# A softmax factor moved: from the product's columns into the exponentials, in a two-layer cross-attention kernel

## The chip, the cores and the metric

The kernel runs on one core of a Trainium2 chip. A core has five engines that work side by side, each through its own list of instructions in order: TensorE (PE in the profile, with its weight loads as PEld), VectorE (DVE), ScalarE (ACT), GpSimd (POOL) and SyncE (SP, which here only issues DMAs). The metric is the device time of one execution in microseconds (us).

## The reference, cut to what matters

Two cross-attention layers, over 4 batches of 1024 rows of 512 features, with a context of 1024 rows of 384 features. All in fp32. Layer 0, which the change touches, has 16 heads of 64:

```python
h = layernorm(x) * gamma + beta
Q, K, V = h @ Wq, context @ Wk, context @ Wv        # 16 heads of 64
attn = softmax(Q @ K^T, axis=-1) * 64 ** -0.5       # the scale stands after the softmax
x = x + (attn @ V) @ Wo + bo
```

Layer 1 has 16 heads of 32, an RMS norm, rotary embeddings and normed queries and keys, `softmax(q @ k^T * sqrt(32)) @ v`, and adds its projection to x in the same way. The change doesn't touch it.

## The kernel before, in words

The outer loop runs over the batches. Within a batch, layer 0 goes through 8 pairs of heads (p), and for each pair through 8 tiles of 128 query rows (i): 64 steps a batch, 256 in all. `Attention0.step` (L381) is one step. Two steps, an even and an odd one, make a block (BQ = 2): 32 blocks a batch, 128 in all.

A step works for the two heads of the pair (j = 0, 1), with 1024 context rows each:

1. `scores` (L372): four matmuls of 64x512 into two PSUM tiles "s" of 128 queries x 1024 context rows. There are two such tiles in all, so the next step's scores need this step's exponentials to have read them.
2. Maxima (L395, VectorE) and exponentials (L396, ScalarE) into e, with the row sums l gathered on the way.
3. A first filling (L398): up to 1.8 us of other work from a list of units (below).
4. Transposes of e in place on VectorE (L401), which turn 32x32 squares; then, in an odd step, 16 DMAs (L407, SP's queue) that carry the squares of the block to their places in eT, so that context rows lie on the partitions. e and eT have two buffers each, and each buffer holds a block.
5. The reciprocals of the row sums (L408), 128x2.
6. In an even step, if two blocks are waiting: `product` (L443) of the older one, 32 matmuls of the values with eT into a PSUM bank av, and then one VectorE multiplication (L456) of av by the factors.
7. A second filling with the rest of the step's share (L416).

The product has heads' features on its partitions and queries along its columns, while the reciprocals have the queries on the partitions. So the factors are turned: `factors` (L418) spreads the reciprocals, times 64 ** -0.5, over 64 columns each on GpSimd (rb), and `factors_turned` (L431) transposes rb on TensorE into a bank rT and copies that to the place of the result (vals) on ScalarE (L441).

The order of work is written out by hand. `Units` holds a list of small pieces of other work, each with a cost in microseconds: projections of the next pairs (k, q, v; matmuls on L158, evacuated by ScalarE copies on L130), output projections that VectorE adds to x (L301), norms, layer 1's first keys with their rotation (L499 to L504) in pairs 6 and 7. `fill` issues pieces until their costs reach what the step is given; the loop (L798 to L809) spreads what is left evenly over the remaining steps, and takes 3.9 (AV) off a step that issues a product. While the first filling runs, rotations are held back (`holds["posts"]`) and issued after the transposes (`flush`). The PSUM banks for fillings, rT and av are four, taken in turn (`bank`).

After a batch's last step two blocks are still without their product. Their products stand in the list of work between layer 0 and layer 1 (L827 to L835), with output projections, the norm of layer 1 and the first queries and keys.

## Time and profile before

| what | value |
|---|---|
| time, median of 3 runs | 2983.13 us (2977.34 to 2984.37) |
| the profiled execution | 2979.04 us, span 2976.8 us |
| TensorE clock granted | 0.997 |
| layer 0 of batch 0, pairs 1 to 5 (96.2 to 364.7 us) | 268.5 us, 40 steps |
| L396 exponential, 128x1024, ACT, x512 | 1109 ns each |
| L395 maximum, 128x1024, DVE, x512 | 1218 ns each |
| L401 transpose, 128x1024, DVE, x512 | 1223 ns each |
| L441 copy of the factors, 128x256, ACT, x128 | 372 ns each |
| L456 product with the factors, 128x256, DVE, x128 | 408 ns each |
| eT DMAs, 128 KB, SP's queue, x2048 | 2.4 us to landing |

A line of the timeline gives the start in us from the span's beginning, the duration, engine, source line, operation, what is written and read, and how many instructions were merged; in square brackets stands the idle time of the engine ahead of it, and what ended it. Instructions that follow one another without a wait overlap by about 0.1 us in the records, so two maxima of 1.22 us take 2.36. A line of the windows gives the stretch, its length, the busy time of each engine with its count of instructions, the clock, the DMA engines' share and GB/s.

### The profile page before, as it was taken

To read this page: it belongs to the slowest core of one execution; us is meant where nothing else is said; L and a number is where in the kernel's file an instruction comes from. 1 tells how busy PE (TensorE), PEld (TensorE's weight loads), DVE (VectorE), ACT (ScalarE), POOL (GpSimd) and SP (SyncE) were. 2 spreads that over 40 slices of the span, in tenths; PEclk is the share of its full clock that TensorE was granted. 3 is DMA by queue.
4 is the path that set the end of the run, shared out by engine and by line. 5 is a ranking of instruction groups with operands and counts; after the bars stand their busy time and mean duration, and the time that the engine had idled before them with its cause. 6 is when DMAs were issued, how large, how long until landed. Compare 5 with 4: busy or idle time off the path is not lost.

```text
span 2976.8 us, 60525 instructions
## 1 busy us (share of the span) xinstructions
PE 2914.2 (98%) x24748; PEld 1541.9 (52%) x24748; DVE 2228.5 (75%) x2824; ACT 1429.5 (48%) x2265; POOL 416.5 (14%) x392
## 2 busy tenths in 40 slices
PE   8999999999999999999999999999999999999998
PEld 5544546555544555655554454555455455555544
DVE  4777795877777779587777777958767777795777
ACT  3444443656534444465644444446664444444664
POOL 0010012420000002232000000223100000023310
PEclk9999999999999999999999999999999999999999
DMA  5787674010388777301048887730104878772000
GB/s 146 169 197 180 158 178 114 21 35 25 74 200 196 183 161 178 95 21 35 25 95 213 183 177 169 166 84 21 35 25 117 209 176 182 167 171 66 2 2 30
DMA packets 177525, 348.49 MB, mean 117 GB/s; under 512 B 37600, under 2 KB 93152, under 8 KB 177248
## 3 DMA queue, kind: packets, MB, share of 16 engines
q1 hardware_dynamic: 175056, 343.43, 48.8%
q8 instruction: 196, 3.21, 0.5%
q10 hardware_dynamic: 2192, 1.19, 0.1%
q14 instruction: 81, 0.66, 0.1%
HBM read 67.64 MB, written 8.39 MB: 26 GB/s over the span
## 4 chain that ended last, share of the span: by engine, by line
PE 82%; DVE 8%; DMA 3%; SPq 3%; ACT 2%; issue 1%; POOL 1%; ACTq 0%; DVEq 0%
PE s L372 15%; PE av L449 13%; PE po L158 10%; PE s L597 7%; PE pv L158 7%; PE av L636 6%; PE pqT L158 6%; PE pkT L158 5%; PE q_p L158 3%; PE av L647 2%; SPq L407 2%; PE k_p L158 2%; DVE both L613 2%; DMA eT<-e 1%; PE rT L440 1%
## 5 line engine op out<-in xcount | busy, mean ns | idle before, releaser
L396 ACT ACTIVATE e<-s,m 128x1024 f32<-128x1024 f32 x512 | 565.6, 1109 | 666.7 <-DVE m L395 623.1
L395 DVE TENSOR_REDUCE m<-s 128x1 f32<-128x1024 f32 x512 | 602.6, 1218 | 321.4 <-PE s L372 321.4
L607 ACT ACTIVATE e<-s 128x1024 f32<-128x1024 f32 x512 | 496.5, 1022 | 315.3 <-PE s L597 300.2
L401 DVE STREAM_TRANSPOSE e<-e 128x1024 f32<-128x1024 f32 x512 | 606.6, 1223 | 46.9 <-ACT e L396 41.1
L372 PE MATMUL s<-qk 64*128 64x512 f32 x2048 | 520.5, 615 | 6.0 <-ACT e L396 5.3
L449 PE MATMUL av<-eT,v 128*64 128x256 f32 x4096 | 470.3, 382 | 7.8 <-DMA eT<-e 6.2
L613 DVE TENSOR_TENSOR both<-e 128x512 f32<-128x512 f32 x512 | 342.1, 699 | 128.9 <-ACT e L607 93.7
L449 PEld LDWEIGHTS av<-eT,v 128*64 128x64 f32 x4096 | 285.5, 137 | 205.3 <-issue 50.2
L372 PEld LDWEIGHTS s<-qk 64*128 64x128 f32 x2048 | 181.8, 186 | 262.6 <-issue 188.5
L597 PE MATMUL s<-q,k 32*128 32x256 f32 x4096 | 304.7, 401 | 5.8 <-ACT q L524 2.7
L597 PEld LDWEIGHTS s<-q,k 32*128 32x128 f32 x4096 | 190.8, 184 | 149.6 <-ACT e L607 71.4
L158 PE MATMUL po<-wo,vals 128*128 128x512 f32 x512 | 239.6, 601 | 2.5 <-ACT v L130 2.5
L158 PE MATMUL pqT<-hT,w 128*128 128x512 f32 (+1 forms) x800 | 241.3, 597 | 0.7 <-ACT hT L255 0.7
L441 ACT COPY vals<-rT 128x256 f32<-128x256 f32 x128 | 47.7, 372 | 327.4 <-PE rT L440 327.4
L301 DVE TENSOR_TENSOR x<-x,po 128x512 f32<-128x512 f32 x200 | 133.6, 678 | 82.6 <-PE po L158 82.6
L158 PEld LDWEIGHTS pv<-w,cT 128*128 128x128 f32 (+1 forms) x2400 | 176.7, 152 | 30.3 <-issue 27.2
L158 PE MATMUL pv<-w,cT 128*128 128x128 f32 (+1 forms) x2400 | 186.5, 275 | 0.0
L158 PE MATMUL pkT<-cT,w 128*128 128x512 f32 (+1 forms) x600 | 182.7, 601 | 1.0 <-ACT cT L130 1.0
L617 DVE TENSOR_TENSOR both<-both 128x1024 f32<-128x1024 f32 x128 | 159.7, 1248 | 4.4
L158 PEld LDWEIGHTS po<-wo,vals 128*128 128x128 f32 x512 | 90.9, 190 | 106.5 <-issue 102.3
L158 PEld LDWEIGHTS pqT<-hT,w 128*128 128x128 f32 (+1 forms) x800 | 85.9, 151 | 112.2 <-issue 105.9
L636 PE MATMUL av<-e,v 128*32 128x256 f32 x2048 | 137.0, 385 | 0.0
(461 smaller groups left out, 2669.9 us busy)
## 6 DMA issues: line engine op xcount, KB each, us to landing
eT<-e SPq DMA_DIRECT2D x2048, 128.0 KB, 2.4
xr<-in_x_dram SPq DMA_DIRECT2D x32, 256.0 KB, 4.0
x<-in_x_dram SPq DMA_DIRECT2D x32, 256.0 KB, 4.0
wo<-in_Wo_dram SPq DMA_DIRECT2D x16, 512.0 KB, 4.0
out_dram<-x SPq DMA_DIRECT2D x32, 256.0 KB, 2.7
w<-in_Wq_dram SPq DMA_DIRECT2D x31, 256.0 KB, 3.9
c<-in_ctx_dram SPq DMA_DIRECT2D x32, 192.0 KB, 3.8
wkv<-in_wkv_dram SPq DMA_DIRECT2D x16, 384.0 KB, 3.3
```

The source lines that it names most:

```text
L158: nc.tensor.matmul(o[rr], lhsT[:, rr], rhs, start=start, stop=stop)
L301: nc.vector.tensor_add(xt[t], xt[t], pp[0])
L372: nc.tensor.matmul(sc[j][:, kb * 512 : (kb + 1) * 512], pr["qT"][r[j], i * P : (i + 1) * P], pr["kT"][r[j], kb * 512 : (kb + 1) * 512], st ...
L395: nc.vector.tensor_reduce(m[:, j : j + 1], sc[j], AX.X, ALU.max, negate=True)
L396: nc.scalar.activation(e[j], sc[j].rearrange("p (g s) -> p g s", g=4), AF.Exp, bias=m[:, j : j + 1], accum_out=l[:, j : j + 1])
L401: nc.vector.transpose(e[j], e[j])
L449: nc.tensor.matmul(av[r[j], :W].rearrange("p (t a i) -> p t a i", t=BQ, a=4), pr["v"][:, k, r[j]], eT[:, j, :, :, k * 32 : (k + 1) * 32], ...
L597: nc.tensor.matmul(sc[j // 2][:, j % 2, c, :], kT[rr, g, k * P : (k + 1) * P], qT[rr, g, qb * WQ : (qb + 1) * WQ], start=True, stop=True,)
L607: nc.scalar.activation(e, sc[u], AF.Exp, scale=float(np.sqrt(np.float32(HD1))))
L613: nc.vector.tensor_add(self.both[:, kk, 2 * u : 2 * u + 2, :], es[u][:, :, 0, :], es[u][:, :, 1, :])
L617: nc.vector.tensor_add(self.both[:, 0], self.both[:, 0], self.both[:, kk])
L636: nc.tensor.matmul(self.av[rr, 0, :], v[g][:, 2 * kk + c, rr], es[j // 2][:, j % 2, c, :], start=first and c == 0, stop=end and c == 1,)
```

## The change

The factors are no longer turned. In each step the reciprocals are taken for each head apart (128x1), ScalarE multiplies each head's exponentials in place by them, and only then do the transposes come. `factors` and `factors_turned` go, with the tiles rb and rT; the bank av is scaled by the constant 64 ** -0.5 by VectorE, in the new `results`, after the transposes. The product of a block stands in the odd step instead of the even one, right behind its scores and ahead of the first filling; the plan of the fillings follows it (AV is taken off odd steps), and other work joins the list at i == 4 instead of 3. After a batch's last step, the two last products come later in the list: the first behind the first half of the output projection and the norm's statistics, the second behind the norm's turning, the first queries and two pieces of keys.

```diff
         def step(self, p, i, pr, us):
...
-            if i % BQ == 0 and len(self.blocks) == 2:
-                self.factors_turned()
+            if i % BQ == BQ - 1 and len(self.blocks) == 2:
+                self.product()
...
+            li = sb.tile([P, 2], F32, tag="li", bufs=3, name=f"li_{n}")
...
             for j in range(2):
+                nc.vector.reciprocal(li[:, j : j + 1], l[:, j : j + 1])
+                nc.scalar.mul(e[j], e[j], li[:, j : j + 1])
+            for j in range(2):
                 nc.vector.transpose(e[j], e[j])
+            self.results()
             flush()
...
-            nc.vector.reciprocal(self.li[:, i % BQ, :], l)
             if i % BQ == BQ - 1:
-                eT = eT.rearrange("p a (t h) s -> p h t a s", h=2)
-                self.blocks.append((p, i // BQ, pr, eT, self.li))
-            elif self.blocks:
-                if len(self.blocks) == 2:
-                    self.product()
-                self.factors()
+                self.blocks.append((p, i // BQ, pr, eT.rearrange("p a (t h) s -> p h t a s", h=2)))
...
         def product(self):
...
-            nc.vector.tensor_mul(o, av[:, :W], o)
+            self.av = av[:, :W], pr["vals"][:, q * W : (q + 1) * W]
+
+        def results(self):
+            if self.av is not None:
+                av, o = self.av
+                nc.vector.tensor_scalar_mul(o, av, HD0**-0.5)
+                self.av = None
...
-                if i == 3:
+                if i == 4:
                     work.add(other)
...
-                now = 0.0 if i % 2 or len(att.blocks) < 2 else AV
+                now = AV if i % 2 and len(att.blocks) == 2 else 0.0
...
-                todo = work.total() + left + later + AV * (n // 2)
+                todo = work.total() + left + later + AV * ((n + 1) // 2)
...
-        att.factors_turned()
-        work.add([(AV, second)] + flat(outs[:4]) + norms[0]["stats"])
-        work.add(k1[0][0] + [(0.2, att.factors_turned)] + norms[0]["apply"] + [(AV, att.product)])
-        work.add(norms[0]["turn"] + q[0][0] + k1[1][0] + k1[0][2] + flat(outs[4:]) + q[0][2])
+        work.add(flat(outs[:4]) + norms[0]["stats"] + [(AV, product)] + k1[0][0] + norms[0]["apply"])
+        work.add(norms[0]["turn"] + q[0][0] + k1[1][0] + [(AV, product)] + k1[0][2] + flat(outs[4:]) + q[0][2])
         work.drain()
```

More of the change, by code (lines that the diff above doesn't have):

```diff
@@ L383, in step @@
             sc = self.scores(p, i, pr)
-            if i % BQ == 0 and len(self.blocks) == 2:
-                self.factors_turned()
+            if i % BQ == BQ - 1 and len(self.blocks) == 2:
+                self.product()
             m = sb.tile([P, 2], F32, tag="m", bufs=3, name=f"m_{n}")
             l = sb.tile([P, 2], F32, tag="l", bufs=3, name=f"l_{n}")
+            li = sb.tile([P, 2], F32, tag="li", bufs=3, name=f"li_{n}")
             if i % BQ == 0:
                 self.e = sb.tile([P, 4, BQ * 2, S // 4], F32, tag="e", bufs=2, name=f"e0_{n}")
-                self.li = sb.tile([P, BQ, 2], F32, tag="li", bufs=4, name=f"li_{n}")
             e = [self.e[:, :, i % BQ * 2 + j, :] for j in range(2)]
@@ L407, in step, with product @@
                         nc.sync.dma_start(eT[32 * g : 32 * (g + 1), q], self.e[32 * q : 32 * (q + 1), g])
-            nc.vector.reciprocal(self.li[:, i % BQ, :], l)
             if i % BQ == BQ - 1:
-                eT = eT.rearrange("p a (t h) s -> p h t a s", h=2)
-                self.blocks.append((p, i // BQ, pr, eT, self.li))
-            elif self.blocks:
-                if len(self.blocks) == 2:
-                    self.product()
-                self.factors()
-            self.u.fill(us - min(us, 1.8))
-        def factors(self):
-            li = self.blocks[0][4]
-            self.rb = sb.tile([P, BQ, P], F32, tag="rb", bufs=2, name=f"rb_{self.blocks[0][:2]}")
-            nc.gpsimd.tensor_scalar(
-                self.rb.rearrange("p t (j d) -> p (t j) d", j=2),
-                li.rearrange("p t j -> p (t j)").unsqueeze(2).to_broadcast([P, 2 * BQ, HD0]),
-                HD0**-0.5,
-                0.0,
-                ALU.mult,
-                ALU.add,
-            )
-        def factors_turned(self):
-            p, q, pr = self.blocks[0][:3]
+                self.blocks.append((p, i // BQ, pr, eT.rearrange("p a (t h) s -> p h t a s", h=2)))
+            self.u.fill(us - min(us, 1.8))
+        def product(self):
+            p, q, pr, eT = self.blocks.popleft()
             W = BQ * P
@@ L436, in factors_turned @@
                 pr["vals"] = sb.tile([P, S], F32, tag="vals", bufs=4, name=f"vals0_{self.b}_{p}")
-            self.o = pr["vals"][:, q * W : (q + 1) * W]
-            rT = bank(f"rT_{self.b}_{p}_{q}")
-            for k in range(BQ):
-                nc.tensor.transpose(rT[:, k * P : (k + 1) * P], self.rb[:, k, :], ident)
-            nc.scalar.copy(self.o, rT[:, :W])
-        def product(self):
-            p, q, pr, eT, _ = self.blocks.popleft()
-            o, W = self.o, BQ * P
             av = bank(f"av_{self.b}_{p}_{q}")
@@ L455, in product @@
                     )
-            nc.vector.tensor_mul(o, av[:, :W], o)
+            self.av = av[:, :W], pr["vals"][:, q * W : (q + 1) * W]
[3 more added lines that the diff above has]
+                nc.vector.tensor_scalar_mul(o, av, HD0**-0.5)
+                self.av = None
     TH = 2
@@ L825, in xattn_kernel, with product @@
         q1 = rotated_chains(qT1, xnT, NQ, lambda k: wq1[:, k, :], f"q1_{b}_1", tmp)
-        def second():
+        def product():
             att.product()
-            att.factors()
-        att.factors_turned()
-        work.add([(AV, second)] + flat(outs[:4]) + norms[0]["stats"])
-        work.add(k1[0][0] + [(0.2, att.factors_turned)] + norms[0]["apply"] + [(AV, att.product)])
-        work.add(norms[0]["turn"] + q[0][0] + k1[1][0] + k1[0][2] + flat(outs[4:]) + q[0][2])
+            att.results()
+        work.add(flat(outs[:4]) + norms[0]["stats"] + [(AV, product)] + k1[0][0] + norms[0]["apply"])
+        work.add(norms[0]["turn"] + q[0][0] + k1[1][0] + [(AV, product)] + k1[0][2] + flat(outs[4:]) + q[0][2])
         work.drain()
```

## The prediction

> **What bounds the kernel now.** First the page's busy times and its chain of work that ended last, then busy times by stage, then one step in order of time, because the change acts inside a step.

> Busy time, and the two lines of the chain:

> ```profile
> PE 2914.2 (98%) x24748; PEld 1541.9 (52%) x24748; DVE 2228.5 (75%) x2824; ACT 1429.5 (48%) x2265; POOL 416.5 (14%) x392
> ...
> PE 82%; DVE 8%; DMA 3%; SPq 3%; ACT 2%; issue 1%; POOL 1%; ACTq 0%; DVEq 0%
> PE s L372 15%; PE av L449 13%; PE po L158 10%; PE s L597 7%; PE pv L158 7%; PE av L636 6%; PE pqT L158 6%; PE pkT L158 5%; PE q_p L158 3%; PE av L647 2%; SPq L407 2%; PE k_p L158 2%; DVE both L613 2%; DMA eT<-e 1%; PE rT L440 1%
> ```

> TensorE sets the time; the factors' transposes (rT) are 1% of it. By stage, with batch 0's layer 0 cut into pairs 1 to 5 (40 steps), pair 6 and pair 7 (8 steps each); the columns are length, then the busy time of PE, PEld, DVE, ACT and POOL:

> ```profile
> 96.20:364.70 268.50, 267.87 (x1425) 136.59 (x1424) 204.48 (x231) 114.82 (x210) 17.53 (x27) 1.00 0.78 181
> 364.70:417.50 52.80, 52.80 (x271) 27.23 (x270) 46.64 (x61) 21.78 (x40) 10.06 (x10) 1.00 0.76 179
> 417.50:475.00 57.50, 56.18 (x295) 31.64 (x295) 48.72 (x62) 24.05 (x48) 10.06 (x10) 1.00 0.70 163
> ```

> A step takes 268.5/40 = 6.71 us with PE full and VectorE 76% busy: it has some 1.6 us of idle time in a step, in pair 6 only 0.8. One step of pair 4 in the timeline:

> ```profile
> 304.73 2.36 DVE L395 TENSOR_REDUCE m<-s 128x1 f32<-128x1024 f32 x2 [1.48 <-PE s L372]
> 306.05 1.11 ACT L396 ACTIVATE e<-s,m 128x1024 f32<-128x1024 f32 x1 [4.94 <-DVE m L395]
> 307.16 1.11 ACT L396 ACTIVATE e<-s,m 128x1024 f32<-128x1024 f32 x1
> 307.29 2.37 DVE L401 STREAM_TRANSPOSE e<-e 128x1024 f32<-128x1024 f32 x2 [0.20 <-ACT e L396]
> 308.25 1.07 ACT L130 COPY v<-pv 128x512 f32<-128x512 f32 x2
> 309.58 0.12 DVE L408 RECIPROCAL li<-l 128x2 f32<-128x2 f32 x1
> ...
> 312.81 2.35 DVE L395 TENSOR_REDUCE m<-s 128x1 f32<-128x1024 f32 x2 [1.22 <-PE s L372]
> ```

> The first transpose starts 2.56 us after the first maximum (R = 304.73), as the first exponential is done by the time the second maximum is. VectorE has finished the step's work at R+4.85 and then waits for the next scores. That wait is the cover which the change spends.

> [...] the trace has one table load, at the start, so the multiply brings none. [...] a square of 512 elements is 633 ns from SBUF (L229), 601 from PSUM (L497).

> **The change, part by part.**

> Multiply. 512 ACTIVATEs of 128x1024 with one pointer[...]. Bounds: 1.02 (L607, no pointer)[...]. That is 2.1 us more a step on ScalarE, which is busy 115 of 268 us in pairs 1 to 5: no throughput limit. But the multiply stands in ScalarE's order after both exponentials and after the evacuations of the step's first filling, and behind it, in VectorE's order, stand both transposes, the results, and the next step's maxima. The new period of VectorE, from R:
> - second exponential over and the next ACT instruction started: 308.25-304.73 = 3.52;
> - first multiply 1.13, then 0.04 to the waiting engine (the transpose at 307.29 began that long after the accumulator was read, 307.25): R+4.69;
> - both transposes until the next instruction, 309.58-307.29 = 2.29; the second multiply starts at R+4.56 and is over by R+5.69, when the first transpose still runs: R+6.98.

> So a step can't be shorter than 6.98 us, 2.13 later than before. The two 128x1 reciprocals lie in the gap, where they cost nothing; without it 0.1 us.

> On top of 6.98 comes what stands in that ring in the instruction order of the changed kernel. Evacuations ahead of the multiplies: 2 to 3 in a pair, 0.54 each (L130, two in 1.07), 1.3 a pair. Scaled results: 4 a pair at 0.33 (L456 now takes 0.41; 0.08 overlaps), 1.3. In pairs 0 to 5, about one addition of po after the transposes, 0.6 (L301 0.68, less overlap). Sum 55.8+3.2 = 59.0 a pair, 7.38 a step.
> Pair 6: 55.8, evacuations 0.5, results 1.3, six additions 3.5, two rotations of keys (five VectorE instructions after the transposes, 2.5 each) 5.1: 66.2. Pair 7: 55.8, 1.5, 1.3, 0.8 and 5.1: 64.5.

> PE does not stop this: its scores for the next step start once the exponentials have released PSUM, about R+3.6, and are ready at about R+5.4, 1.6 us before VectorE comes. PE has work of some 6.5 us a step (the 6.71 less half of a block's 0.37), so it idles.

> Against before. Batch 0: pair 0 is PE-bound at 69.9 us for 8 steps, stays so and gains 1 us. Pairs 1 to 5: 40 x (7.38-6.71) = 27. A later batch (pairs 0 and 1: 106.9 us, 2 to 5: 220.3): 48 steps in 327.2 = 6.82, 48 x 0.56 = 27. Pair 6: 66.2-52.8 = 13.4. Pair 7: 64.5-57.5 = 7. Four batches: 4 x (27+13.4+7) - 1 = 189.

> Removed: 256 transposes on PE, 0.37 us a block on the chain, 128 x 0.37 = 47 us; 128 ACT copies of 0.37, 128 POOL operations of 0.40, a VectorE product that becomes a scaling. PE's 47 us would come off the time if PE still set it; under the ring above they only lengthen PE's idle time, so I count nothing but the 1 us in pair 0.

> Product a step later. It now follows the scores of an odd step. Exponentials reach eT 2.1 us later, the product waits a step (7 us) longer: nothing. A block's 16 DMAs are issued in some 10 to 11 us (one block's in 11.38) and land 2.4 us after the last; then its e buffer may be written again, by the first exponential three steps on. From the end of the transposes that is 3 x 6.71 + 1.32 - 4.85 = 16.6 us before and 3 x 7.38 + 1.32 - 6.98 = 16.5 after: the late start and the longer steps cancel, and there are 3 to 4 us to spare as before. But 46 of the 512 exponentials waited for this in the trace of before, 31.3 us in all, and where PE set the pace that was partly hidden; in the ring it isn't. Between 0 and 31 us; taken 8. SP's queue holds the same issues in the same order, POOL loses the broadcast alone.

> Last products of a batch. The same PE work between layer 0 and 1, in another order: the first additions (6.9 us) and first keys come ahead of products that used to open the stage. The last transposes come 2.1 us later, but the last product has 21 us of PE work ahead of it, where it had 13. Squares and norm keep their cover (3.7+2.6 us). Between -2 and +2 a batch, taken 0. Layer 1 is untouched.

> The profiled execution took 2979.0 us (span 2976.8), 4 below the median: 2983+189+8 = 3180.

> **Rivals.**
> - A, shorter ring: multiply at L607's 1.02, half of the evacuations hidden because PSUM was ready earlier: 0.2 us x 248 steps = 50 less, 3130. For: the bounds. Against: the evacuation is in order ahead of the multiply whenever its data came.
> - B, longer ring: waits between engines add a quarter of a us, or PE's 1.6 us of lead is lost in steps with much filling: 0.25 x 248 = 60 more, 3240. For: PE's odd steps now hold scores and a product of 3.67 us ahead of any filling.
> - C, e buffer: the DMA engines are 78% busy in this stage, and blocks land too late in most cases, 1.5 us in two thirds of 120 blocks: +120, 3300. For: 46 waits already. Against: the spare time above.
> - D, the other side: VectorE's waits are covered and PE stays the bound: 2983-47 = 2936. It decides where the ring is under PE's 6.5 us, that is, if the multiply with its extras took below 0.4 us. Against: 1024 elements in that time would be twice the rate of any ACT row.
> - E, the scores' lead hides nearly all and both effects cancel: 2980.

> **How the numbers follow.** Forecast 0.60, A 0.17, B 0.12, C 0.06, D 0.03, E 0.02. The range takes in the forecast with its bounds, most of A and B: 3100 to 3245. Some 0.3% is what can be told from no change. Faster D, 0.03; same E, 0.02; slower the rest, 0.95.

> **What would show it.** Right: VectorE waits about 2 us before each first transpose, released by ACT's multiply; maxima no longer wait for scores; PE waits for exponentials at its scores in layer 0; steps of 7.4 us; pair 6 above 65; layer 1 unchanged. Wrong: transposes that start at R+2.6; a multiply well under 1 us; exponentials waiting on DMA in most blocks.

## The result, and the profile after

The changed kernel takes 3209.53 us (median; 3203.41 to 3212.41), the kernel before, beside it, 2983.75. The ratio is 1.0763, 95% interval 1.0745 to 1.0781: 226 us slower, where 197 were forecast. Its profiled execution has a span of 3208.5 us. One execution of the run e9_deferred_product_even below took 11913.12 us, some four times the others, and is left out of that run's median.

Busy times and the chain of work that ended last, of the changed kernel's page (its lines: maxima L397, exponentials L398, reciprocals L403, multiply L404, transposes L406, scaled results L438, scores L374):

```profile
PE 3063.8 (95%) x24492; PEld 1594.9 (50%) x24492; DVE 2277.3 (71%) x3080; ACT 1922.3 (60%) x2649; POOL 366.2 (11%) x264
...
PE 53%; DVE 21%; ACT 11%; SPq 6%; DMA 6%; issue 2%; POOL 1%; ACTq 0%; DVEq 0%
DVE e L406 10%; PE s L374 8%; PE s L580 7%; ACT e L398 7%; PE po L159 6%; PE av L426 6%; PE av L619 6%; SPq L413 6%; PE pv L159 5%; DMA eT<-e 4%; PE pqT L159 4%; DVE m L397 3%; ACT e L404 3%; PE q_p L159 3%; PE pkT L159 3%
```

TensorE's share of the chain fell from 82% to 53%; transposes, exponentials and multiplies took most of it, and the DMAs with their issue went from 6% to 12%. PE still reads 95% busy, though it has fewer instructions than before. The same 2048 score matmuls read 673.9 us busy in place of 520.5, and their weight loads wait 252.5 us for exponentials, where they waited 37.3. In pairs 1 to 5 of batch 0 the granted clock is 1.00 in both kernels, and these matmuls read 107.3 us busy in place of 80.1: some of PE's waiting stands inside what is called busy. A busy share alone would have shown little.

One step of pair 4 in the timeline of the changed kernel:

```profile
283.58 2.34 DVE L397 TENSOR_REDUCE m<-s 128x1 f32<-128x1024 f32 x2
284.82 1.11 ACT L398 ACTIVATE e<-s,m 128x1024 f32<-128x1024 f32 x1 [3.11 <-DVE m L397]
285.95 1.11 ACT L398 ACTIVATE e<-s,m 128x1024 f32<-128x1024 f32 x1
286.06 0.16 DVE L403 RECIPROCAL li<-l 128x1 f32<-128x1 f32 x1
...
287.06 2.17 ACT L404 ACTIVATE e<-e,li 128x1024 f32<-128x1024 f32 x2
287.19 0.16 DVE L403 RECIPROCAL li<-l 128x1 f32<-128x1 f32 x1 [0.97 <-ACT e L398]
...
288.23 2.37 DVE L406 STREAM_TRANSPOSE e<-e 128x1024 f32<-128x1024 f32 x2 [0.87 <-ACT e L404]
290.52 0.39 DVE L438 TENSOR_SCALAR vals<-av 128x256 f32<-128x256 f32 x1
290.83 1.21 DVE L397 TENSOR_REDUCE m<-s 128x1 f32<-128x1024 f32 x1
```

From the first maximum (283.58) the first multiply starts at +3.48, the first transpose at +4.65, and VectorE has done both at +6.94; then the results, and the next maxima at +7.25 with no wait in front. The forecast had +3.52, +4.69 and +6.98. The brackets are the change's price: VectorE waits 0.97 for the second exponential and 0.87 for the multiply. Over the whole run, from VectorE's waits:

```profile
DVE li L403 <- ACT e L398: 217.7, 243, 1.5
DVE e L406 <- ACT e L404: 173.9, 165, 3.3
...
DVE e L406 <- DMA eT<-e: 97.1, 91, 1.4
...
DVE m L397 <- PE s L374: 24.4, 13, 3.4
```

A line of the waits gives the total in us, how often, and the longest. The line that names a DMA is the multiply as well: in all 256 steps the first transpose starts 31 to 34 ns after the end of the first multiply, whichever of the two is named. Maxima wait 24.4 us for scores now; in the kernel before it was

```profile
DVE m L395 <- PE s L372: 321.4, 219, 5.2
```

The stages of batch 0, as the windows of the changed kernel (length, then busy PE, PEld, DVE, ACT, POOL, the granted clock, the DMA share, GB/s):

```profile
95.20:389.60 294.40, 291.49 (x1384) 144.00 (x1383) 210.68 (x271) 190.36 (x269) 10.15 (x8) 1.00 0.73 165
389.60:460.10 70.50, 58.75 (x257) 27.60 (x256) 50.38 (x71) 38.66 (x55) 8.45 (x6) 0.95 0.59 138
460.10:519.40 59.30, 52.85 (x241) 29.43 (x240) 45.38 (x63) 35.73 (x53) 8.45 (x6) 0.91 0.62 143
```

Pairs 1 to 5 (40 steps) take 294.4 us, forecast 295; pair 6 takes 70.5, forecast 66.2. The third window holds the first seven steps of pair 7. From the starts of the score matmuls, batch 0 against before: pairs 0 to 5 364.2 us for 338.4, pair 6 70.5 for 52.8, and from pair 7 to the next batch's first scores 371.4 for 357.4, that is 25.8 + 17.7 + 14.0 = 57.5 us, in four batches 230. The span grew by 231.7.

Of PE's waits, the first of these has grown (it was 5.3 us), as the forecast said. The other two are new, and lie where the forecast was short:

```profile
PE s L374 <- ACT e L398: 57.5, 45, 3.4
PE po L159 <- DVE rot L484: 24.5, 4, 6.4
...
PE pth L254 <- DVE xn L243: 15.2, 4, 3.8
```

Each of the two comes once a batch: in pair 6 an output projection waits for a rotation of keys to have read its PSUM bank, and between the layers the turning of the norm waits for VectorE.

### The profile page after: what moved, and what is told of

Same layout as the page of the kernel before. It is cut to its first block, busy times and chain, and to the rows that moved or that the text cites. A ratio compares the mean times of both kernels' runs of the same rounds, so it can differ in the third digit from the quotient of the medians.

```text
span 3208.5 us, 60142 instructions
## 1 busy us (share of the span) xinstructions
PE 3063.8 (95%) x24492; PEld 1594.9 (50%) x24492; DVE 2277.3 (71%) x3080; ACT 1922.3 (60%) x2649; POOL 366.2 (11%) x264
## 4 chain that ended last, share of the span: by engine, by line
PE 53%; DVE 21%; ACT 11%; SPq 6%; DMA 6%; issue 2%; POOL 1%; ACTq 0%; DVEq 0%
DVE e L406 10%; PE s L374 8%; PE s L580 7%; ACT e L398 7%; PE po L159 6%; PE av L426 6%; PE av L619 6%; SPq L413 6%; PE pv L159 5%; DMA eT<-e 4%; PE pqT L159 4%; DVE m L397 3%; ACT e L404 3%; PE q_p L159 3%; PE pkT L159 3%
## 5 line engine op out<-in xcount | busy, mean ns | idle before, releaser
L398 ACT ACTIVATE e<-s,m 128x1024 f32<-128x1024 f32 x512 | 570.4, 1114 | 731.7 <-DVE m L397 711.1
L406 DVE STREAM_TRANSPOSE e<-e 128x1024 f32<-128x1024 f32 x512 | 607.0, 1224 | 271.0 <-ACT e L404 173.9
L374 PE MATMUL s<-qk 64*128 64x512 f32 x2048 | 673.9, 640 | 59.2 <-ACT e L398 57.5
L397 DVE TENSOR_REDUCE m<-s 128x1 f32<-128x1024 f32 x512 | 597.3, 1205 | 24.4 <-PE s L374 24.4
L404 ACT ACTIVATE e<-e,li 128x1024 f32<-128x1024 f32 x512 | 558.5, 1141 | 6.1 <-DVE li L403 5.4
L374 PEld LDWEIGHTS s<-qk 64*128 64x128 f32 x2048 | 248.6, 191 | 423.2 <-ACT e L398 252.5
L159 PE MATMUL po<-wo,vals 128*128 128x512 f32 x512 | 247.6, 617 | 24.5 <-DVE rot L484 24.5
L403 DVE RECIPROCAL li<-l 128x1 f32<-128x1 f32 x512 | 82.0, 162 | 244.3 <-ACT e L398 217.7
```

The costliest lines, as they stand in the source:

```text
L159: nc.tensor.matmul(o[rr], lhsT[:, rr], rhs, start=start, stop=stop)
L374: nc.tensor.matmul(sc[j][:, kb * 512 : (kb + 1) * 512], pr["qT"][r[j], i * P : (i + 1) * P], pr["kT"][r[j], kb * 512 : (kb + 1) * 512], st ...
L397: nc.vector.tensor_reduce(m[:, j : j + 1], sc[j], AX.X, ALU.max, negate=True)
L398: nc.scalar.activation(e[j], sc[j].rearrange("p (g s) -> p g s", g=4), AF.Exp, bias=m[:, j : j + 1], accum_out=l[:, j : j + 1])
L404: nc.scalar.mul(e[j], e[j], li[:, j : j + 1])
L406: nc.vector.transpose(e[j], e[j])
```

## The experiments

All times are medians, beside runs of the kernel before on the same chip (2980.3 to 2982.6 us in these groups, 2983.75 beside the changed kernel), so a difference between two groups is uncertain by some 3 us. The kernels of e1, e2, e11 and e12 leave out the division by the row sums, that of e5 half of it; the others compute all of it. Times of a pair are of batch 0 unless said otherwise.

| run | us | ratio to before, interval |
|---|---|---|
| e1_no_multiply | 3087.91 | 1.0359 (1.0336 to 1.0382) |
| e2_multiply_aside | 3088.91 | 1.0365 (1.0338 to 1.0393) |
| e3_even_transposes_later | 3095.28 | 1.0381 (1.0360 to 1.0401) |
| e5_half_multiply | 3140.82 | 1.0538 (1.0519 to 1.0557) |
| e6_product_even | 3255.25 | 1.0909 (1.0882 to 1.0935) |
| e9_deferred_product_even | 3040.86 | 1.0191 (1.0166 to 1.0216) |
| e10_deferred_no_hold | 3087.80 | 1.0351 (1.0331 to 1.0371) |
| e11_no_multiply_late_reciprocals | 3040.66 | 1.0189 (1.0161 to 1.0217) |
| e4_multiply_first | 3176.80 | 1.0657 (1.0636 to 1.0678) |
| e7_no_hold | 3195.38 | 1.0719 (1.0703 to 1.0735) |
| e8_last_products_back | 3186.56 | 1.0686 (1.0665 to 1.0706) |
| e12_only_factors_gone | 2962.05 | 0.9928 (0.9911 to 0.9945) |

**The multiply taken out.**

```diff
                 nc.vector.reciprocal(li[:, j : j + 1], l[:, j : j + 1])
-                nc.scalar.mul(e[j], e[j], li[:, j : j + 1])
```

> The changed kernel without the multiply: the exponentials stay undivided, all else is as it was, so the computation lacks the division by the row sums. Ring (the multiply holds the transposes, and those the next maxima): VectorE is free at R+4.9 again, PE sets the pace, the 47 us of the removed transposes show: 2925 to 2955 us. Rival, the moved products or the e buffers cost the time: stays near 3200.

3088: the multiply is worth 121 us, and both theories miss. The ring alone would have given everything back; the rest is something else in the change. VectorE's timeline of this run, in pair 6:

```profile
395.35 2.34 DVE L397 TENSOR_REDUCE m<-s 128x1 f32<-128x1024 f32 x2
397.88 0.16 DVE L403 RECIPROCAL li<-l 128x1 f32<-128x1 f32 x1 [0.19 <-ACT e L398]
398.97 0.16 DVE L403 RECIPROCAL li<-l 128x1 f32<-128x1 f32 x1 [0.93 <-ACT e L398]
399.38 2.37 DVE L405 STREAM_TRANSPOSE e<-e 128x1024 f32<-128x1024 f32 x2 [0.24 <-DMA eT<-e]
```

The first transpose starts 4.03 us after the first maximum, 2.56 in the kernel before: the second reciprocal stands ahead of it in VectorE's order and waits for the second exponential. (The last 0.24 us, put down to a DMA, is 0.21 to 0.24 us in nearly every step that has it, so a late transfer is hardly what it is.) A shorter ring is left, of about 6.3 us (4.03 + 2.29), an estimate. It is hidden under PE in pairs 3 and 5 (53.9 and 54.5 us, 54.6 and 53.9 before), but not in pair 6 (62.7) and 7 (58.0 for seven steps, before 50.4), where rotations lengthen it. Pair 4 is longer too (58.0 us, 55.5 before); there exponentials wait 8.1 us for the DMAs that still read the e buffer, 77.9 us over the whole run where it was 31.3.

**The same work on ScalarE, off the ring.**

```diff
-                nc.scalar.mul(e[j], e[j], li[:, j : j + 1])
+                for _ in range(2):
+                    nc.scalar.mul(aside, aside, li[:, j : j + 1])
```

Here aside is a tile of 128x512 that nobody reads.

> The changed kernel with ScalarE's multiplies done on a tile of their own that nobody reads (four of 128x512 in a step, 2.8 us of ScalarE where the change has 2.3), and the exponentials undivided: the division is left out. Ring: the work is there, but no transpose waits for it: 2925 to 2970 us, like the one without the multiply. Rival, ScalarE's load: evacuations and exponentials come late behind 2.8 us a step, 3200 or more.

3089, as without the multiply, with this group among those of the run:

```profile
L407 ACT ACTIVATE aside<-aside,li 128x512 f32<-128x512 f32 x1024 | 737.8, 721 | 57.1 <-DVE li L405 32.1
```

That is 4 x 0.721 = 2.9 us a step. 738 us more of ScalarE cost nothing that can be measured. ScalarE's load is out as a cause; what costs is that the transposes wait.

**Transposes of the even step in the odd step's gap.**

```diff
+            def factor(j):                      # the reciprocal and the multiply of head j
+                ...
+            if i % BQ:
+                for j in range(2):
+                    nc.vector.transpose(self.even[j], self.even[j])
+                    factor(j)
             ...                                 # the first filling
+            if i % BQ == 0:
+                factor(0), factor(1)
+                self.even = e
+            else:
+                for j in range(2):
+                    nc.vector.transpose(e[j], e[j])
```

> The changed kernel with the transposes of an even step put behind the maxima of the odd step that follows; nothing is left out. Ring: those transposes fill the gap in which VectorE waits for the odd step's multiply, two steps need 12.4 us of the ring where PE needs 13: 2935 to 2990 us, under the kernel before unless the e buffers' DMAs, which start 2 us later than before, hold up exponentials. Rival, load of ScalarE or the products' places: 3150 or more, since neither is altered.

3095, so 114 us come back with the full computation, nearly all that leaving the multiply out gives. In pairs 3 and 5 the steps are at PE's pace again (53.9 and 54.2 us). Pairs 6 and 7 keep the same excess as in e1 (63.5, and 59.1 for seven steps), which again is not the multiply.

**Half of the multiply** (the first two of e's four column groups only):

```diff
-                nc.scalar.mul(e[j], e[j], li[:, j : j + 1])
+                nc.scalar.mul(e[j][:, :2], e[j][:, :2], li[:, j : j + 1])
```

> The changed kernel with the multiply on half of the columns (128x512 of 128x1024), so half of the exponentials stay undivided. Ring: only the first multiply's length is in the period, 0.43 us shorter, over some 248 steps 107 us: about 3100. Rival, load: both multiplies count, twice that, where ScalarE sets the pace: about 3000. A price for waiting alone, whatever the length: 3200.

3141, 69 us less, against 107. In pair 6, 70.6 us become 66.8, and in pair 1, 57.8 become 54.3: all of the ring's 8 x 0.42 = 3.4 (the 1141 ns of L404 less the 721 of a 128x512 in e2, an estimate). In pair 3 it is 2.8, in the seven steps of pair 7 only 0.8. So the length of one multiply a step counts, where the ring is the bound; what stops the gain elsewhere was not isolated.

**The product back in the even step.**

```diff
-            if i % BQ == BQ - 1 and len(self.blocks) == 2:
-                self.product()
...
                 self.blocks.append(...)
+            elif len(self.blocks) == 2:
+                self.product()
+                self.results()
...
-                now = AV if i % 2 and len(att.blocks) == 2 else 0.0
+                now = 0.0 if i % 2 or len(att.blocks) < 2 else AV
```

> The changed kernel with the product, its budget and its results put back into the even step, where they stood before; the multiply stays. Theory 1, two causes: the multiply's ring costs some 120 us (3209 to 3088 without it) and the other 105 us come from the product's place, which leaves all filling to even steps, so that PE stops for a PSUM bank in pair 6: then this takes off pair 6's stall, 4 x 5 us and some of pair 7: 3150 to 3190. Theory 2, the rest comes from the reciprocals ahead of the transposes, which wait for the second exponential: the same time, 3200 to 3215.

3255, 46 us slower: wrong for both. Beside the multiply, the odd step is the better place. The stop that was to go comes twice a batch instead, from PE's waits of this run:

```profile
PE po L159 <- DVE rot L485: 50.0, 8, 7.3
```

So that stop is not tied to the product's place alone, but to how late VectorE reads the bank.

**Deferred transposes, and the products back in all their old places** (the edits of e3 and e6, `i == 3` for other work, and the last two products as before):

> The even step's transposes behind the odd step's maxima, as in the run before, and the product, its budget, the last two products and the joining of other work back in their places of before; ScalarE's multiply stays, nothing is left out. Theory 1: the ring is gone and the bank stall too: 2935 to 2985. Theory 2: the odd step still has its reciprocals ahead of its transposes: pair 6 and 7 stay long, 3060 to 3095. If products now wait for the later DMAs: between.

3041, 54 less than e3, between the two theories. Pairs 6 and 7 are 57.6 and 55.6, and the stretch to the next batch is back at 304.9 (before 306.9, e3 311.2). But pair 2 rises from 55.4 to 59.1 (in the later batches pairs 1 and 2 are longer, too), and the waits point to what the expectation had named, the products that wait for DMAs; from ScalarE's and PE's waits:

```profile
ACT e L396 <- DMA eT<-e: 68.3, 17, 5.9
```

```profile
PE av L437 <- DMA eT<-e: 29.6, 12, 4.8
```

The exponentials' wait is as long in e3 (66.4 us); PE's is not there at all, so it is the new one. That it makes up the whole rise isn't shown. It is the fastest kernel with the multiply on ScalarE here, and still 1.9% slower than the one before.

**Deferred transposes, rotations not held back** (e3 without the two lines that set `holds`):

> The even step's transposes behind the odd step's maxima, and the rotations of keys in pairs 6 and 7 no longer held back until after the transposes; products as in the changed kernel, nothing is left out. Theory 1: the bank that PE waits for in pair 6 is read some 5 us earlier, no stop there: pair 6 from 62 to under 57, 3060 or less. Theory 2: no difference, 3085 to 3100.

3088 against 3095, which were not measured side by side: unclear, near no difference. Pair 6 falls from 63.5 to 62.2 in batch 0. PE's wait for a rotation falls from 16.8 to 7.2 us. In an even step of e3 no transposes stand between, which would explain that the holding did little there.

**No multiply, and the reciprocals behind the transposes.**

```diff
             for j in range(2):
-                nc.vector.reciprocal(li[:, j : j + 1], l[:, j : j + 1])
-                nc.scalar.mul(e[j], e[j], li[:, j : j + 1])
-            for j in range(2):
                 nc.vector.transpose(e[j], e[j])
+            for j in range(2):
+                nc.vector.reciprocal(li[:, j : j + 1], l[:, j : j + 1])
```

> The changed kernel without the multiply (the division by the row sums is left out) and with the reciprocals behind the transposes, so that the first transpose waits for the first exponential only, as before. Theory 1: pairs 6 and 7 stay 8 to 10 us longer than before, since the product's place is the same: 3060 to 3090. Theory 2: they go back to 53 and 50 us: 2930 to 2980.

3041, 47 less than e1. Pair 6 goes from 62.7 to 56.8 and the seven steps of pair 7 from 58.0 to 53.6. So the reciprocals' wait is a cost of its own, of 47 us, which stands hidden behind the multiply as long as that is there. The 47 us are net of what came in their place: exponentials now wait 157.9 us for the DMAs of e, 77.9 in e1. The 79 us between this run and e12 (below) are the new places of the products and of other work.

**The multiply ahead of the first filling** (the two lines moved above `fill`):

> The changed kernel with reciprocals and multiplies ahead of the first filling, so that the evacuations stand behind the multiplies on ScalarE; nothing is left out. Ring with the evacuations in it, as forecast (0.54 us each, 1.3 a pair): 31 pairs x 1.3 = 40 less, about 3170. If evacuations are hidden somewhere: 3205 to 3212.

3177, 33 less (forecast 40): evacuations between the exponentials and the multiply were in the ring, at nearly the price used.

**Rotations not held back, in the changed kernel** (without the two lines that set `holds`):

> The changed kernel with the rotations of keys in pairs 6 and 7 not held back until after the transposes. If PE's stop in pair 6 is for a PSUM bank that the held rotation still has to read, and the rotations lengthen the ring behind the transposes: they now lie in VectorE's gap, pair 6 falls from 71 to some 63 and pair 7 by 3 to 5, 4 x 11 = 45 less, about 3165, and the half-clock stretches at the end of layer 0 get fewer. If the stop has another cause: 3200 to 3215.

3195, 14 less, a third of what was expected. The wait of po for a rotation is gone from PE's waits, and pair 6 falls from 70.6 to 66.7 us in batch 0. Pair 7 does not gain (61.3 for seven steps, 59.3 with the holding). The mean granted clock is 0.982, with the holding 0.978. The cause of the stop is shown. That a rotation which lies in the gap costs more than was read would explain the rest; no run isolates it.

**The last two products back.**

```diff
-        work.add(flat(outs[:4]) + norms[0]["stats"] + [(AV, product)] + k1[0][0] + norms[0]["apply"])
-        work.add(norms[0]["turn"] + q[0][0] + k1[1][0] + [(AV, product)] + k1[0][2] + flat(outs[4:]) + q[0][2])
+        work.add([(AV, product)] + flat(outs[:4]) + norms[0]["stats"] + k1[0][0] + norms[0]["apply"] + [(AV, product)])
+        work.add(norms[0]["turn"] + q[0][0] + k1[1][0] + k1[0][2] + flat(outs[4:]) + q[0][2])
```

> The changed kernel with the last two products of a batch back in their old places in the list (the first ahead of the output projections, the second behind the norm's apply). If their new place costs the 5.8 us that lie between the last step of layer 0 and the next batch: 4 x 5.8 = 23 less, about 3186. If that stretch is longer for the late transposes or the clock instead: 3205 to 3215.

3187, 23 less, as expected. PE and VectorE between the layers, first in the changed kernel:

```profile
538.64 2.86 PE L159 MATMUL k_p<-wkv,cT 128*128 128x256 f32 x12
...
542.16 0.69 DVE L482 TENSOR_TENSOR rot<-k_p,cos 128x512 f32<-128x512 f32 x1 [2.98 <-ACT rot L480]
...
544.76 1.66 DVE L243 TENSOR_SCALAR xn<-x,rs 128x512 f32<-128x512 f32 x4
...
545.29 4.14 PE L254 MATMUL pth<-ident,xn 128*128 128x128 f32 x16 [3.79 <-DVE xn L243]
```

and PE in this run:

```profile
537.70 2.75 PE L159 MATMUL k_p<-wkv,cT 128*128 128x256 f32 x12
...
541.19 3.67 PE L426 MATMUL av<-eT,v 128*64 128x256 f32 x32 [0.74 <-DMA eT<-e]
...
544.80 2.27 PE L254 MATMUL pth<-ident,xn 128*128 128x128 f32 x16
```

The old place put a product of 3.67 us over the time in which VectorE rotates the keys and applies the norm. Without it PE stands idle for 3.79 us, and the 16 transposes that follow take 4.14 us instead of 2.27.

**Only the factors gone** (e11 with the edits of e6, `i == 3`, and the last products back):

> No multiply and late reciprocals, as in the run of that name, and besides the product, its budget, the last products and the joining of other work back in their old places: the kernel before without its factors (rb, their transposes and copies), so the division by the row sums is left out. If PE sets the pace, as the prediction read the kernel before, and the removed transposes are worth 0.37 us a block: 2981 - 47 = 2935, 2925 to 2950. Then the 105 us between this and the run without multiply and with late reciprocals (3041) belong to the new places of the products: 23 to the last two, 80 to the others. If 2970 to 2990: the removed transposes were worth nothing even there. Above 3000: something else of the change costs it.

2962, a gain of 20 us over the kernel before, between the two readings. Pairs 3 to 5 are 0.7, 1.6 and 0.8 us shorter, where 1.5 each was due. Exponentials wait four times as long for e's DMAs as before (31.3 us):

```profile
ACT e L396 <- DMA eT<-e: 120.2, 32, 5.4
```

That fits a gain lost to the DMAs, but no run took that wait away alone, say by a third e buffer, so it stays argued. Another part is PE's clock: in batches 1 to 3 one step of pair 7 takes 9.8 to 10.0 us, 6.6 in batch 0. In batch 1, after a stop of 1.55 us, the clock granted from 1159.6 to 1162.3 us is 0.50, and the product after it takes 5.37 us in place of 3.67. In the three batches together these steps are some 10 us longer, of the 27 that are missing from the 47; the mean granted clock, 0.995 in this run's profiled execution and 0.997 in the kernel before's, puts the clock's part at some 6 (0.002 x 2962), an estimate.

Taken off one after the other, the change's 226 us are: multiply 121 (3209.5 to 3087.9), the reciprocals' wait 47 (to 3040.7), the products' and other work's new places 79 (to 2962.1), and the removed factors -20 (to 2982, the kernel before in that group). Each share carries the DMA waits and the clock that come or go with its step, and the shares depend on the order: with the multiply in place, the product's old step costs 46 more, not less.

## Why the prediction was right, and where it was short

- **The ring was the mechanism, and its length was right.** 6.98 us forecast, 6.94 measured; 59.0 us for a pair, 294.4/5 = 58.9 measured. The forecast's 1.13 us for a multiply was the author's estimate, and the page's group of L404 has 1141 ns. The trace of before comes to 1109 + 32 = 1141 ns, an estimate, from L396, of the same size with one pointer, and from what the square from SBUF (L229, 633 ns) takes more than the one from PSUM (L497, 601 ns), though of these two only L229 also gathers a sum. Both traces have one table load, of 1.28 us, at the start, so the multiply brought none. In pairs 6 and 7 the ring is not all. Without the multiply (e1) they still lie 9.8 and 7.6 us above the kernel before (the latter for seven steps), where the changed kernel lies 17.7 and 8.9 above it. Other bounds stand close under the ring there, so that the forecast's 13.4 and 7 us came as near as they did is in part luck.
- **"The two 128x1 reciprocals lie in the gap, where they cost nothing; without it 0.1 us."** The first half is true as the change stands. The 0.1 us counts only how long they run: they are also a second tie of the transposes to the second exponential, and once the multiply is away, that wait costs 47 us.
- **Pair 6, 66.2.** Measured 70.5. The missing term is the stop of PE for a PSUM bank (6.4 us once a batch), which the sum didn't look for: it priced how late the rotation makes VectorE, and not who waits for what the rotation reads. Without holding (e7) the stop is gone and pair 6 took 66.7, but that run also moves the rotation out of the ring, so its nearness to 66.2 isn't a check of the sum.
- **"Last products of a batch ... taken 0."** It cost 23 us. The step that failed is "Squares and norm keep their cover (3.7+2.6 us)": the sum counted the work ahead of the norm's apply, but the keys' rotation stands there on VectorE too, and the product that had covered it, behind the apply, was moved away.
- **"Product a step later ... nothing."** With the ring in place its old step is slower (e6), so as a part of this change it cost nothing or gained. Without the ring, the new places of all products and of the other work cost 79 us; 23 is what the last two cost in e8.
- **PE's 47 us "only lengthen PE's idle time".** Consistent with the stages; even without the ring they are worth 20 us and not 47, so rival D's 2936 was out of reach for a second reason.
- **The e buffer, 8 us.** Exponentials wait 13.5 us for these DMAs in the changed kernel, 4 times, where they waited 31.3 before, 46 times: the term was too high, and rival C is out. The wait grows where the ring is shorter or gone: 77.9 us in e1, 66.4 in e3, 68.3 in e9, 120.2 in e12, 157.9 in e11.
- **The sum.** Redone with the spans of the profiled executions, over four batches: pair 6 is 18 us longer than forecast, the stretch from pair 7 to the next batch 31 (23 of it the last products), pairs 0 to 5 are some 5 shorter, and the 8 of the e buffer did not come. That is 36; the span grew by 231.7 us against 197, which is 35 more. (Between the medians the miss is 29, as the profiled execution of the kernel before lies some 5 us below its median.) It happens to lie near rival B's 3240, but for neither of B's two reasons: the wait from the multiply to the transpose was 0.03 us, where 0.04 were read, and PE's lead held (maxima waited 24 us for scores in all).

## What to carry to other kernels

An operation with free capacity on its own engine can still lengthen the kernel (here ScalarE was 48% busy before and 60% after, for 226 us more), if a third engine's list stands behind its result: add up the ring that goes through all of them, from one maximum to the next, and compare that with the bound engine's work in a step. Then look at each place where the order changed for what it had covered: a product that looks movable may be the only work over another engine's chain. And a wait that costs nothing beside a longer one (here the reciprocals', 47 us) comes out when the longer one is repaired, so a repair should be priced with both.

## What the runs showed of the hardware

```profile
441.89 1.88 PE L159 MATMUL po<-wo,vals 128*128 128x512 f32 x4
...
450.60 3.47 PE L159 MATMUL po<-wo,vals 128*128 128x512 f32 x4 [6.40 <-DVE rot L484]
```

After 6.40 us of idleness they take 3.47 us in place of 1.88. The clock granted in these 3.47 us is 0.56, and 1.00 in the 2.9 us after them. After the 3.79 us between the layers 16 transposes take 4.14 instead of 2.27, at a granted clock of 0.59. The length of a stop doesn't tell alone what follows it, as these two lines of the changed kernel show, the first of pair 6:

```profile
437.44 3.11 PE L374 MATMUL s<-qk 64*128 64x512 f32 x8 [2.32 <-ACT e L398]
...
1653.87 4.80 PE L374 MATMUL s<-qk 64*128 64x512 f32 x8 [1.25 <-ACT e L398]
```

In the 3.11 us after the stop of 2.32 the granted clock is 1.00, in the 4.80 after the one of 1.25 it is 0.63. What else decides, these runs don't show.

The mean granted clock of the profiled executions is 0.997 before, 0.978 in the changed kernel, 0.987 in e11 and 0.995 in e12. In pair 6 of the changed kernel it was 0.95, in seven steps of pair 7 0.91. The share that was not granted is 0.022 x 3208.5 = 71 us of the changed kernel's span and 0.003 x 2976.8 = 9 of the other's. So the clock took at most some 71 us, an estimate, against at most 9 before, and less where PE had nothing to do anyway.
